# Two key tiles to a step: regrouped attention and turned mean squares in the first layer of a three-part kernel

## The chip, the cores and the metric

The kernel runs on one core of a Trainium2 chip. A core has a matrix engine (TensorE, PE in the profile, with its weight loads listed apart as PEld), three engines for element-wise work (VectorE or DVE, ScalarE or ACT, GpSimd or POOL) and a queue engine (SyncE, SP) that issues the transfers here. Each engine takes its instructions in order. Operands lie in the on-chip memory SBUF, matrix products in the small memory PSUM, of eight banks.

The metric is the device time of one execution in microseconds (us); several executions are summed up by their median. A profile is one further execution with every instruction recorded; its own time is given beside it.

## The reference, cut to what matters

The input is x, 8 batches of 256 channels on a 32 x 32 grid (1024 positions). Three parts follow: layer 0 (attention over the grid plus a gated convolution network with an 8 x 8 FFT filter), layer 1's causal attention, and layer 1's eight experts. Only layer 0 is touched, and the place where it hands over to layer 1:

```python
def _ln(x, w, b):
    r = lax.rsqrt(jnp.mean(x * x, axis=1, keepdims=True) + LN_EPS)
    return x * r * w[:, None, None] + b[:, None, None]

# attention: 4 heads, keys of 32, values of 64 channels
qkv = _bn(_conv1x1(x, qkv_w), ...)
attn = softmax(einsum('bhkn,bhkm->bhnm', q, k) * SCALE)
out = einsum('bhdm,bhnm->bhdn', v, attn) + _bn(_dwconv3(v_img, pe_w), ...)
return _bn(_conv1x1(out, proj_w), ...)

# EDFFN
x = _dwconv3(_conv1x1(x, pi_w), dw_w)        # 1024 channels
x = gelu(x1) * x2                            # 512 channels
x = _conv1x1(x, po_w)
x = irfft2(rfft2(8x8 patches of x) * fft_p)

# layer 0
x = x + gamma1 * attention(_ln(x, norm1))
x = x + gamma2 * edffn(_ln(x, norm2))
```

All is in float32.

## The kernel before, in words

**Engines and order.** All of layer 0's compute goes through the wrapper `InOrder` (line 59; the recorded call is line 69, which is why every row of the profile says L69). Each engine runs in the order in which the program text issues its instructions, so the weaving described below decides what stands behind what. Rows are told apart by their tiles.

**Tiles.** PSUM is divided into `ps_s` (two tiles of two banks, tag s: the scores `s`, the products `pz`, and some of `pq` and `pp`), `ps_o` (the attention's `po` and `sums`) and `ps_m` (two banks in turn, tag mm, for all the rest).

**The pieces of one batch's work.** The names are those of the profile's tiles.

- `rms_norm` (line 571) makes the normed input `xn`, in two halves of 512 positions. ACT squares (`sq`). PE multiplies each 128 positions of the squares, as the stationary operand, with a column `mean_1` (`ms`, 16 instructions a half). ACT copies to `y`, POOL makes the power -0.5, one Newton step and a split into two parts (`a`, `y`, `r`, a chain on 128x4). PE transposes (`tr`), ACT copies (`rT`), PE spreads the row over all partitions (`rbn`), and DVE multiplies (`xn`).
- `queries_keys` (line 649): norm1, then the products `pq` for queries and keys, split by ACT into a high part `hi` and by DVE into a rest `lo`. `stack` (line 671) copies these parts, one transfer of 128 KB for each head and part, into `qst` and `kst`, in which the high and low parts of a head's 32 channels lie on 128 partitions; one matmul then gives the score to full precision.
- `values` (line 684): `pq` again, `vfull`, transposes `tpv` into `vT`, and the padded picture `vpad`.
- `v_conv` (line 714): the 3 x 3 convolution of the values on DVE, 16 "taps" of 128x1024 into `o`.
- `attend` (line 723): four chunks of 256 queries times eight key tiles of 128 keys. Each step makes one key tile's `s` (4 matmuls, one per head) and its exp `pT` (ACT), then the products `po` and `sums` of the key tile before it. po and sums write 32 columns each, four instructions beside one another on column tiles of the array. When a chunk is complete, `close` copies its results and returns a list of later steps, taken one to a key tile: `invert` (DVE reciprocal `sr`), `split` (ACT `rh`, POOL `rl`), `spread` (PE `rb`; DVE two operations, pu and o).
- `finish` (the last chunk's steps) and `project` (line 813): products `pp`, added to the residual `t` by DVE.
- `hidden` (line 884): the EDFFN's first part for the batch before: `ph` on PE, the padded `hpad` on ACT, eight taps of 128x1024 on DVE for each of eight groups (tiles `x` and `conv`), gelu on ACT, and the product `hid` on DVE (two rows to a group).
- `spectrum` (line 975), for the batch two before: `pz` from `hid`, `zf`, `pf` (the DFT), `gf` (DVE filter), `py` (inverse) and the DVE addition to `t`.

**The order.** `main_of(i)` weaves generators: the head is norm2(i-1) alternating with spectrum(i-2), and one step of the head's weave in every three is followed by a step of attend(i); the rest of attend(i) is woven with queries_keys(i+1), one step of it to every two of attention; then finish, gelu, stack, values(i+1) and project(i). `together` runs this main chain beside a side chain, v_conv(i) followed by hidden(i-1), choosing between them by the sums of the numbers that each generator yields: a yield is an estimate of the us of the work since the last, and the chain that is behind goes next. For i = 1 and 7 the side's numbers are scaled by 0.75.

Two places in a steady batch are used as marks. One is the point at which `pz` starts again for spectrum(i-2) after its wait for the last `hid`; the other is the `rb` of chunk 2, behind which DVE has the o update, a run of taps, the reciprocal of chunk 3 and the last `hid` products.

Of the kernel before, what the change touches and what calls it, by code (L numbers as in the profile page):

```python
# [18 lines left out]
P = 128  # L19
B, C, H, W = 8, 256, 32, 32  # L20
N = H * W
# [34 lines left out]
NVEC = _n  # L56

# [17 lines left out]
def conv_attn_hybrid_kernel(  # L75
# [29 lines left out]

    vec = const.tile([P, NVEC], F32, name="vec")
    nc.sync.dma_start(vec, vecs)

    def col(name, i=0, n=1):
        o, w = _VOFF[name]  # L110
        assert i + n <= w
        return vec[:, o + i : o + i + n]
# [6 lines left out]
    mean_1 = const.tile([P, 1], F32, name="mean_1")  # L119
    nc.gpsimd.memset(mean_1, 1.0 / C)  # L120

# [310 lines left out]
    with ExitStack() as l0:  # L432
# [97 lines left out]
        pick_n = wpool.tile([2 * nq, nq, P], F32R, name="pick_n")  # L530
        pickn = one.tile([2 * nq, nq, P], F32, tag="full", name="pickn", bufs=2)
        nc.gpsimd.memset(pickn, 0.0)
        for half in range(2):
            nc.gpsimd.affine_select(
                out=pickn, in_=pickn, compare_op=ALU.not_equal, fill=1.0, base=-nq * half,
                pattern=[[-1, nq], [0, P]], channel_multiplier=1,
            )
        nc.gpsimd.tensor_copy(pick_n, pickn)
        mhalf = const.tile([P, nq], F32, name="mhalf")
# [6 lines left out]
        def padded(name):  # L546
            p = one.tile([P, H + 2, W + 2], F32, tag=name, name=name)
            nc.gpsimd.memset(p, 0.0)
            return p

# [3 lines left out]
        def interior(p, h):  # L554
            r = H // 2
            return p[:, 1 + h * r : 1 + (h + 1) * r, 1 : 1 + W]
# [4 lines left out]
        def tap(dst, p, w, k):  # L561
            src = p[:, k // 3 : k // 3 + H, k % 3 : k % 3 + W]
# [6 lines left out]
        def rms_norm(b, wname, xn):  # L569


            sq_of, r_of, rT_of = {}, {}, {}

            def squares(h):
                sq_of[h] = []
                for k in range(KC):
                    sq = one.tile([P, HALF], F32, tag="full", name="sq", bufs=2)
                    act.activation(sq, t[b][:, k, h * HALF : (h + 1) * HALF], AF.Square)
                    sq_of[h].append(sq)

            def factors(h):
                ms = ps_m.tile([P, nq], F32, tag="mm", name="ms")
                for k, sq in enumerate(sq_of.pop(h)):
                    for i in range(nq):
                        pe.matmul(
                            ms[:, i : i + 1], sq[:, i * P : (i + 1) * P], mean_1,
                            start=(k == 0 and i == 0), stop=(k == KC - 1 and i == nq - 1),
                        )
                y = small.tile([P, nq], F32, tag="y", name="y")
                act.activation(y, ms, AF.Identity, bias=eps_rms)  # L590

                r = r_of[h] = small.tile([P, 2, nq], F32, tag="r", name="r")
                a = small.tile([P, nq], F32, tag="a", name="a")
                pool.tensor_tensor(a, y, mhalf, ALU.pow)
# [4 lines left out]
                pool.tensor_copy(r[:, 0, :].bitcast(F32R), a)  # L599
                pool.tensor_sub(r[:, 1, :].bitcast(F32R), a, r[:, 0, :])  # L600

            def turned(h):
                tr = ps_m.tile([2 * nq, P], F32, tag="mm", name="tr")
                pe.transpose(tr, r_of.pop(h).rearrange("p a b -> p (a b)"), ident)
                rT_of[h] = small.tile([2 * nq, P], F32R, tag="rT", name="rT", bufs=2)
                act.copy(rT_of[h], tr)

            def apply(h):
                rT = rT_of.pop(h)
                rb = ps_m.tile([P, HALF], F32, tag="mm", name="rbn")  # L610
                for i in range(nq):
                    pe.matmul(rb[:, i * P : (i + 1) * P], pick_n[:, i, :], rT, start=True, stop=True)
# [6 lines left out]
            factors(0)  # L619
            squares(1)  # L620
            yield 2.0
            factors(1)
            yield 2.0
            turned(0)
            yield 0.2
            apply(0)
            turned(1)
            yield 1.0
            apply(1)
            yield 1.0  # L630
# [21 lines left out]
        def queries_keys(b):  # L652
# [7 lines left out]
            for g in range(2):  # L660
                hi = one.tile([P, N], F32R, tag=f"hi{g}", name="hi")
                lo = one.tile([P, N], F32, tag=f"lo{g}", name="lo")
# [7 lines left out]
                att[b][g] = (hi, lo)  # L670
# [1119 lines left out]
```

## Time and profile before

| what | value |
|---|---|
| median of 3 runs | 3320.35 us (3318.31 to 3326.01) |
| the profiled execution's own time | 3326.09 us |
| its span in the profile | 3324.3 us |
| mean granted TensorE clock | 0.969 |
| layer 0 | 0 to about 1444 us |
| layer 1's attention, then the experts | to about 2080 us, then to the end |
| PE, DVE, ACT, POOL busy | 94%, 72%, 43%, 10% |
| transfers | 113.85 MB, mean 34 GB/s |

The span runs from the first instruction to the last; 1.8 us of the profiled execution lie around it. A row of the timeline is a run of equal instructions: start, duration, engine, line, operation, output<-inputs, shapes, count, and in brackets how long the engine had been idle just before and what it waited for. Since matmuls overlap, the starts of successive PE rows say more than their durations. A row of windows gives, for a stretch of time, each engine's busy time with its number of instructions, then the granted TensorE clock as a share of full speed, the share of the transfer engines and GB/s.

### The profile page before, as it was taken

To read this page: it belongs to the slowest core of one execution; us is meant where nothing else is said; L and a number is where in the kernel's file an instruction comes from. 1 tells how busy PE (TensorE), PEld (TensorE's weight loads), DVE (VectorE), ACT (ScalarE), POOL (GpSimd) and SP (SyncE) were. 2 spreads that over 40 slices of the span, in tenths; PEclk is the share of its full clock that TensorE was granted. 3 is DMA by queue.
4 is the path that set the end of the run, shared out by engine and by line. 5 is a ranking of instruction groups with operands and counts; after the bars stand their busy time and mean duration, and the time that the engine had idled before them with its cause. 6 is when DMAs were issued, how large, how long until landed. Compare 5 with 4: busy or idle time off the path is not lost.

```text
span 3324.3 us, 43278 instructions
## 1 busy us (share of the span) xinstructions
PE 3108.8 (94%) x17366; PEld 2108.0 (63%) x17366; DVE 2395.9 (72%) x3710; ACT 1417.6 (43%) x2185; POOL 328.9 (10%) x530
## 2 busy tenths in 40 slices
PE   6998999999999998769999998999999999999999
PEld 4554646464656555345556666687878777878787
DVE  2369788878787887744554444688888877888887
ACT  2545454555454544313333332344444444444443
POOL 1120101020202010001222222400000000000000
PEclk9989999999999999879999999899999999999999
DMA  4112020202020200030111101100000000000000
GB/s 121 29 24 51 26 52 26 51 27 51 27 51 26 52 14 7 16 134 13 51 47 43 39 26 45 45 25 21 20 20 20 24 18 26 23 20 26 13 7 13
DMA packets 42918, 113.85 MB, mean 34 GB/s; under 512 B 6406, under 2 KB 14550, under 8 KB 38870
## 3 DMA queue, kind: packets, MB, share of 16 engines
q1 hardware_dynamic: 42710, 111.01, 11.0%
q8 instruction: 139, 2.28, 0.3%
q14 instruction: 69, 0.57, 0.1%
HBM read 43.61 MB, written 33.82 MB: 23 GB/s over the span
## 4 chain that ended last, share of the span: by engine, by line
PE 50%; DVE 4%; ACT 1%; POOL 1%; issue 0%; DMA 0%; POOLq 0%; ACTq 0%; SPq 0%; DVEq 0%
PE pm L69 12%; PE pa L69 12%; PE q L69 11%; PE s L69 5%; PE po L69 3%; PE pv L69 2%; PE pk L69 2%; DVE zt L69 1%; DVE nm L69 1%; PE tpt L69 1%; DVE pr L69 1%; PE tp L69 1%; ACT pr L69 1%; PE tpz L69 1%; PE pw L69 1%
## 5 line engine op out<-in xcount | busy, mean ns | idle before, releaser
L69 ACT ACTIVATE h<-h,bn_o,bn_s 128x512 f32<-128x512 f32 x384 | 308.7, 813 | 632.5 <-DVE h L69 632.4
L69 DVE SCALAR_TENSOR_TENSOR conv<-hpad,vec,conv 128x1024 f32<-128x1024 f32 x256 | 331.4, 1300 | 14.7 <-ACT conv L69 8.9
L69 DVE SCALAR_TENSOR_TENSOR x<-hpad,vec,x 128x1024 f32<-128x1024 f32 x248 | 321.6, 1300 | 23.5 <-ACT x L69 17.4
L69 ACT ACTIVATE pT<-s 128x1024 f32<-128x1024 f32 x256 | 261.6, 1024 | 150.3 <-PE s L69 150.1
L69 PE MATMUL pm<-h,w 128*128 128x512 f32 (+1 forms) x768 | 318.1, 523 | 0.0
L69 PE MATMUL po<-pT,vT 128*32 128x256 f32 x4096 | 276.5, 388 | 6.5 <-ACT pT L69 4.8
L69 PE MATMUL ph<-xn,piw 128*128 128x512 f32 x512 | 246.1, 608 | 3.1 <-DVE gf L69 1.1
L69 PE MATMUL s<-kk,z 128*128 128x512 f32 x512 | 242.4, 601 | 0.6 <-DVE pr L69 0.6
L69 PE MATMUL s<-qst,kst 128*128 128x256 f32 x1024 | 217.9, 335 | 6.1 <-DMA kst<-lo 5.9
L69 PEld LDWEIGHTS s<-qst,kst 128*128 128x128 f32 x1024 | 147.8, 192 | 88.8 <-issue 72.2
L69 PEld LDWEIGHTS pm<-h,w 128*128 128x128 f32 x768 | 146.7, 191 | 75.6 <-issue 62.1
L69 DVE TENSOR_TENSOR h<-h,wb 128x1024 f32<-128x1024 f32 x128 | 156.8, 1225 | 43.2 <-ACT h L69 43.2
L69 DVE TENSOR_TENSOR h<-pa,first 128x512 f32<-128x512 f32 x128 | 88.3, 690 | 134.9 <-PE pa L69 131.4
L69 DVE SCALAR_TENSOR_TENSOR o<-vpad,pe_w,o 128x1024 f32<-128x1024 f32 x128 | 163.3, 1281 | 24.1 <-ACT o L69 21.2
L69 ACT ACTIVATE hpad<-ph,pi_o 128x512 f32<-128x512 f32 x126 | 87.0, 691 | 211.7 <-PE ph L69 207.2
L69 DVE TENSOR_TENSOR h<-h,first 128x256 f32<-128x256 f32 x384 | 164.3, 428 | 13.2
L69 PEld LDWEIGHTS po<-pT,vT 128*32 128x32 f32 x4096 | 107.7, 109 | 88.7 <-ACT pT L69 8.3
L69 PEld LDWEIGHTS ph<-xn,piw 128*128 128x128 f32 x512 | 90.8, 190 | 108.9 <-issue 92.1
L69 PE MATMUL sums<-pT,ones 128*32 128x256 f32 x2048 | 158.8, 382 | 0.0
L69 PE MATMUL pz<-pow__118,hid 128*128 128x256 f32 x512 | 129.8, 408 | 29.1 <-DVE hid L69 29.1
L69 PE MATMUL pa<-tz,ws 128*128 128x256 f32 x512 | 156.0, 387 | 0.0
L69 PE MATMUL pa<-ze,w 128*128 128x256 f32 x512 | 153.8, 383 | 0.0
(258 smaller groups left out, 5940.3 us busy)
## 6 DMA issues: line engine op xcount, KB each, us to landing
t<-in_x_dram SPq DMA_DIRECT2D x8, 1024.0 KB, 7.5
qst<-hi SPq DMA_DIRECT2D x64, 128.0 KB, 2.3
qst<-lo SPq DMA_DIRECT2D x64, 128.0 KB, 2.3
kst<-hi SPq DMA_DIRECT2D x64, 128.0 KB, 2.3
kst<-lo SPq DMA_DIRECT2D x64, 128.0 KB, 2.3
td<-t SPq DMA_DIRECT2D x8, 1024.0 KB, 3.8
t<-td SPq DMA_DIRECT2D x8, 1024.0 KB, 4.9
ze<-zd SPq DMA_DIRECT2D x16, 512.0 KB, 4.1
```

The costliest lines, as they stand in the source:

```text
L69: return self._tc.keep_in_program_order(method(*args, **kwargs))
```

## The change

1. `attend` takes two key tiles to a step: both `s` tiles and both exps are issued, then the products of the two key tiles before them. `pT` gets four buffers instead of two. A chunk's later steps come one to a step of two tiles, so the list loses its empty places. The yields become 3.5 and 2.6.
2. `rms_norm`: the squares are now the moving operand and 32 columns of ones the stationary one, in four column tiles for the four 128-position parts, so that mean squares of both halves stand in one bank as rows, each repeated over 32 partitions. ACT scales and copies this block (`yr`, 128x256, in `level`), PE transposes its halves (`tpy`), one ACT copy takes one column per part (`y`), and one POOL chain on 128x8 serves both halves. One pair of `tr`, one `rT`, then both `rbn` and the four DVE products follow together. norm2 has one more empty step ahead of `tr`.
3. `hi` and `lo` have one buffer each for both groups; their parts go to DRAM (four writes of 512 KB a batch) and `stack` reads them back in eight transfers of 512 KB.
4. The padded pictures have rows of 33 instead of 34 columns, one column of zeros serving as the right border of a row and the left one of the next.
5. `vec`, the table of small parameters, is loaded in two parts. The second, with the parameters of the experts, is loaded behind layer 0, and its batch-norm factors are computed there too, instead of at the start.
6. The weave constants: the head gives attention a step every 6 instead of every 3, queries_keys a step to each step of attention (of two tiles now) with one instead of two empty steps ahead; v_conv's yield in `hidden` is 1.7 instead of 1.5.

The steps a steady batch issues on DVE keep their number, but not their places. Behind the o update of chunk 2, DVE's order held, before, 16 taps, the reciprocal, the o update of chunk 3, three pairs of hid products and one pair of additions of pp ahead of the last pair of hid; after, 20 taps and two pairs of additions.

The diff, cut to its core:

```diff
-    vec = const.tile([P, NVEC], F32, name="vec")
-    nc.sync.dma_start(vec, vecs)
+    vec = const.tile([P, NVEC0], F32, name="vec")
+    nc.sync.dma_start(vec, vecs[:, :NVEC0])
...
-            p = one.tile([P, H + 2, W + 2], F32, tag=name, name=name)
+            p = one.tile([P, (H + 2) * (W + 1) + 2], F32, tag=name, name=name)
...
-            src = p[:, k // 3 : k // 3 + H, k % 3 : k % 3 + W]
+            src = inside(p, k // 3, k % 3, H)
...
+            def means(h):
+                if h == 0:
+                    of["ms"] = ps_m.tile([P, 2, P], F32, tag="mm", name="ms")
+                for k, sq in enumerate(of.pop(h)):
                     for i in range(nq):
                         pe.matmul(
-                            ms[:, i : i + 1], sq[:, i * P : (i + 1) * P], mean_1,
-                            start=(k == 0 and i == 0), stop=(k == KC - 1 and i == nq - 1),
+                            of["ms"][i * KD : (i + 1) * KD, h, :], ones[:, :KD], sq[:, i * P : (i + 1) * P],
+                            start=(k == 0), stop=(k == KC - 1),
                         )
+            def level():
+                of["yr"] = one.tile([P, 2, P], F32, tag="yr", name="yr")
+                act.activation(of["yr"], of.pop("ms"), AF.Identity, bias=eps_rms, scale=1.0 / C)
+
+            def factors():
+                yr = of.pop("yr")
+                tp = ps_m.tile([P, 2, P], F32, tag="mm", name="tpy")
+                for h in range(2):
+                    pe.transpose(tp[:, h, :], yr[:, h, :], ident)
+                y = small.tile([P, 2, nq], F32, tag="y", name="y")
+                act.copy(y, tp[:, :, ::KD])
...
             squares(0)
             yield 0.2
-            factors(0)
+            means(0)
             squares(1)
-            yield 2.0
-            factors(1)
-            yield 2.0
-            turned(0)
+            yield 1.0
+            means(1)
+            level()
+            yield 1.0
+            factors()
+            yield 1.0
+            for _ in range(gaps):
+                yield 1.0
+            turned()
             yield 0.2
             apply(0)
-            turned(1)
-            yield 1.0
             apply(1)
-            yield 1.0
+            yield 2.0
...
-                att[b][g] = (hi, lo)
+                parts = att[b][g] = [dram.tile([P, N], F32, tag=f"part{g}{r}", name="part", bufs=2) for r in range(2)]
+                for part, src in zip(parts, (hi, lo)):
+                    nc.sync.dma_start(part, src.bitcast(F32))
...
-                    for hd in range(NH):
-                        nc.sync.dma_start(
-                            st[r * KD : (r + 1) * KD, hd, :].bitcast(F32), src[hd * KD : (hd + 1) * KD, :].bitcast(F32)
-                        )
+                    nc.sync.dma_start(
+                        st[r * KD : (r + 1) * KD].bitcast(F32), src.rearrange("(h k) n -> k h n", k=KD)
+                    )
...
-                return [None, invert, None, split, None, None, spread]
+                return [invert, split, None, spread]
...
+                for j0 in range(0, nj, 2):
+                    new = []
+                    for j in (j0, j0 + 1):
+                        ks = slice(j * P, (j + 1) * P)
+                        s = ps_s.tile([P, NH, QC], F32, tag="s", name="s")
+                        for hd in range(NH):
+                            pe.matmul(s[:, hd, :], kst[:, hd, ks], qst[:, hd, qs], start=True, stop=True)
+                        pT = two.tile([P, NH, QC], F32, tag="pT", name="pT", bufs=4)
+                        act.activation(pT, s, AF.Exp)
+                        new.append((po, sm, j, pT, c))
+                    products()
+                    late.extend(new)
                     later()
-                    yield 1.75
+                    yield 3.5
...
-            yield from rms_norm(b, "n2w", xn2[b])
+            yield from rms_norm(b, "n2w", xn2[b], 1)
...
-                yield 1.5 * us
+                yield 1.7 * us
...
-                yield from weave(head, steps, 3, rest=False)
-            yield from weave(steps, later_on(2, queries_keys(i + 1)) if i + 1 < B else none(), 2)
+                yield from weave(head, steps, 6, rest=False)
+            yield from weave(steps, later_on(1, queries_keys(i + 1)) if i + 1 < B else none(), 1)
```

## The prediction

> **What bounds the kernel now.** I read the page first, then windows by stage, then PE and DVE row by row inside one batch, then the ends of waits. The page gives TensorE most of the span and VectorE three quarters:
>
> ```profile
> span 3324.3 us, 43278 instructions
> ...
> PE 3108.8 (94%) x17366; PEld 2108.0 (63%) x17366; DVE 2395.9 (72%) x3710; ACT 1417.6 (43%) x2185; POOL 328.9 (10%) x530
> ```
>
> That mean hides two kinds of stretch. Layer 0 ends near 1444 us and repeats every 163.65 us (the same DVE row at 475.14 and 638.78). The windows (start:end, length, busy time of PE, PEld, DVE, ACT, POOL, then clock, DMA share, GB/s) cut one batch, i=3, at two marks: pz restarting after its wait for hid, and the rb of chunk 2.
>
> ```profile
> 501.96:631.86 129.90, 126.08 (x1107) 76.44 (x1107) 104.42 (x98) 66.84 (x100) 20.08 (x31) 1.00 0.05 17
> 631.86:665.61 33.75, 28.69 (x127) 14.56 (x123) 31.27 (x32) 18.24 (x30) 0.84 (x1) 0.90 0.55 125
> ```
>
> For 129.90 us PE is the bound (it waits 3.8 us, DVE 25). In the next 33.75 us, the transition, DVE is the bound (idle 2.5): it finishes the side work on which the next pz depends. So time saved on PE counts in the first, and VectorE work pushed past the mark counts in full in the second. Batch 1 (DVE 58.64 of 60.00 us from 240 on) is DVE's; i=0 (PE 80.49 of 81.00 from 72 on) is PE's.
>
> PE's rows show a key tile (start, duration):
>
> ```profile
> 586.59 0.74 PE L69 MATMUL s<-qst,kst 128*128 128x256 f32 x4
> 587.26 1.07 PE L69 MATMUL po<-pT,vT 128*32 128x256 f32 x16
> 588.15 0.61 PE L69 MATMUL sums<-pT,ones 128*32 128x256 f32 x8
> 588.70 1.99 PE L69 MATMUL ph<-xn,piw 128*128 128x512 f32 x4
> ...
> 633.00 1.07 PE L69 MATMUL po<-pT,vT 128*32 128x256 f32 x16
> 633.89 0.61 PE L69 MATMUL sums<-pT,ones 128*32 128x256 f32 x8
> 634.32 1.05 PE L69 MATMUL po<-pT,vT 128*32 128x256 f32 x16
> 635.18 0.61 PE L69 MATMUL sums<-pT,ones 128*32 128x256 f32 x8
> 635.73 1.98 PE L69 MATMUL ph<-xn,piw 128*128 128x512 f32 x4
> ```
>
> Starts matter: s to po 0.67, po to sums 0.89, sums to the next kind 0.55, together 2.11 us; at 633 two products stand together, and there sums to po takes 0.43.
>
> Last, what a wait at pz does. Batch 2 restarts at 332.04 after 3.41 us; batch 7 after 0.69:
>
> ```profile
> 332.04 4.63 PE L69 MATMUL pz<-pow__118,hid 128*128 128x256 f32 x10 [3.41 <-DVE hid L69]
> 336.46 3.41 PE L69 MATMUL ms<-mean,sq 128*128 128x1 f32 x16
> ```
> ```profile
> 1158.11 2.42 PE L69 MATMUL pz<-pow__118,hid 128*128 128x256 f32 x10 [0.69 <-DVE hid L69]
> 1160.37 1.84 PE L69 MATMUL ms<-mean,sq 128*128 128x1 f32 x16
> ```
> ```profile
> 332.10:345.10 13.00, 13.00 (x41) 0.50 0.00 0
> 332.04:346.30 14.26, 14.26 (x46) 0.55 0.00 0
> 1158.11:1166.08 7.97, 7.97 (x46) 1.00 0.01 2
> ```
>
> The same 46 matmuls take 14.26 us in place of 7.97: after the wait the granted clock (third figure from the right) is 0.50 for 13 us. That is 6.3 us lost in a PE-bound stretch, and batch 2 (332.04 to 501.96) is 169.92 long, 6.27 over the period.
>
> **The change part by part, per steady batch.**
>
> *Steps of two tiles.* A pair costs 2 x 2.11 = 4.22 us. Afterwards: s to s 0.46 (estimate: 4 instructions at the 0.115 us between the starts of the three rb at 632.08, 632.19 and 632.31, of the same shape), s to po 0.67, then 0.89 + 0.43 + 0.86 + 0.55 as at 633; 3.86, so 0.36 saved; bounds 0.15 (only the 633 rows) and 0.42. The exps (1.02 us each) get two more pT buffers, so products wait less for ACT. 14 of a batch's 16 pairs lie before the mark: -5.0 (-2.1 to -5.9). One more s stands ahead of the mark: +0.45.
>
> *Mean squares.* A half is 16 instructions in 1.84 us (1160.37). Now 32 ones are loaded instead of 128 squares, and 16 instructions run in four column tiles of 128 columns; nearest is sums, 8 instructions with 256 columns in 0.43 to 0.55. I take 0.85 (0.6 to 1.2): four halves a batch (norm2, and norm1 of the next), -4.0 (-2.6 to -5.0). Two added transposes per norm at 0.14 us (tpv's 273 ns rows overlap, four in 0.44-0.6): +0.55. mean_1's memset goes, once.
>
> *The norm's chain.* ms goes through level (128x256 on ACT, some 0.4 us, ss's row), tpy, the copy y, and one POOL chain of 128x8 for both halves; tr waits for POOL on PE, with s, products, rbn and pz queued behind it. Rows of the old chains:
>
> ```profile
> 506.45 2.08 POOL L69 TENSOR_TENSOR a<-y,mhalf 128x4 f32<-128x4 f32 x1 [16.66 <-ACT y L69]
> ...
> 513.49 1.01 POOL L69 TENSOR_TENSOR a<-y,mhalf 128x4 f32<-128x4 f32 x1
> ...
> 517.94 0.20 POOL L69 TENSOR_TENSOR r<-a,r 128x4 fp32r<-128x4 f32 x1
> ```
>
> 7.0 and 4.65 us beside DVE's taps; without them 2.66 (570.58 to 573.24). The 128x8 pow is 1.67 us (layer 1, 1464.01) against 1.01, so 3.3 quiet, 5.3 to 7.8 beside taps; I take 6.4. Behind y, PE has pz(2) (3.5) but only once the first exp frees an s tile, then pf: some 3.1 us of cover. tr waits 3.3 (2 to 4.7). The third pf waits about 1.0, others 1.0; the stretch's waits go from 3.8 to 5.3: +1.5.
>
> So the PE-bound stretch changes by -5.0 + 0.45 - 4.0 + 0.55 + 1.5 = -6.5, to 123.4.
>
> *DVE behind the mark.* The weaves' constants and v_conv's 1.5 to 1.7 reorder DVE's program order. Before, 16 taps follow chunk 2's o update; after, 20, and one more pair of t<-pp stands ahead of the last hid: 4 x 1.28 + 1.4 - 1.2 (fewer waits inside) = +5.3 (4 to 6.5), transition 39.1. DVE loses that work in a stretch where it has 25 us to spare, so nothing comes back. PE's pp ends near 32, six pz follow, and pz then waits for hid about 5.4 us instead of 0.7.
>
> *The clock.* 5.4 us is longer than the 3.41 that halved the clock at 332, so I expect it at every restart. Lost: pz's ten 4.63 - 2.42 = 2.2, then, with the slow ms gone, part of the next sixteen pz (5.6 against 3.6) before the clock returns: I take 3.4 (0 if no drop; 6.3 as at 332).
>
> The Trainium skill, TensorE: Matmul & The Clock Gate, section "What's actually happening", lets the full clock return after one busy window of some 3.4 us. By it a restart would lose about 1.7 us (an estimate from that page) and the sum below would be 9 us lower; the 13 us at 332 contradict it, and I go by the trace.
>
> *Stacking.* 4 writes of 512 KB and 8 reads instead of 32 copies of 128 KB, all on SP's queue. In the loop s(i+1) starts 48 us after them: hidden; without that cover some 10 us. hi and lo have one buffer, so group 1 waits for group 0's writes (2.8 us for 512 KB). At the start it is open:
>
> ```profile
> 71.12 3.36 PE L69 MATMUL s<-qst,kst 128*128 128x256 f32 x8 [5.91 <-DMA kst<-lo]
> ```
>
> 2 MB at the 208 GB/s of that copy against writes landing and 2 MB at the 400 to 420 of a DRAM read, one landing more, the buffer's wait, and -1.8 for the norm: 0 (-5 to +5).
>
> *Little or nothing:* 33-column pads (every tap is 1.28 us, at each of the three column offsets); level's larger ACT row (ACT is busy 51% of that stretch); vec's second part as one more DMA on SP's queue behind layer 0 (8 KB of wrs beside it land in 2.5 us) and the moved bn fold, one ACT table load of 1.28 us and ten small rows: +0.5 at layer 1's start, up to 4 if PE finds nothing else there.
>
> **Sum.** Start 0; i=0: 15 pairs x 0.36 and 2 halves x 1.0, -7.5; i=1, DVE-bound, -1; i=2: -6.5 + 5.3 + 3.4 - 6.3 (its halved clock is there already) = -4.1; i=3 to 6: 4 x (-6.5 + 5.3 + 3.4 = +2.2) = +8.8; i=7, DVE-bound from 1192 on, part of its slow restart: +2; norm2 at the end -2; layer 1 +0.5. Total -3.3. The profiled execution took 3326.1 (span 3324.3 and 1.8 around it), so 3322.8; it lies 5.7 above the median of the runs, 3320.35, from which the forecast is 3317: gain and loss cancel.
>
> **Rivals.**
> *A, slower: the halved clock stays.* Place: pz's restart in i=3 to 7. If it holds for 13 us as at 332, a restart loses 6.3, not 3.4: 5.5 x 2.9 = +16, 3333. Beyond 5.2 us per restart it passes the measurement's bound. For it: row 332.04. Against: in the transition at 652.2 half clock ended after 6.8 us, and ms, at half clock 3.41 of those 13 us, shrinks.
> *B, faster: no drop.* If pz's wait stays short enough for full clock (pp ending later than 32 on a half clock of its own): -3.4 x 5.5 = -19, 3298. For it: 0.7 us now leaves the clock full; against: 3.41 did not.
> *C, faster: the transition does not lengthen,* because DVE runs those taps in waits I have not seen: -5.3 x 5 and with it B, about 3272. Against: DVE idles 2.5 us there.
>
> **How the numbers follow.** Forecast 0.40, A 0.27, B 0.23, C 0.10. The median of three runs spans 0.2%, 6.6 us, about what a measurement can tell from no change. Within the forecast's case the pair saving alone moves the sum by 0.2 x 88 pairs = 18 us one way, 5 the other, and tr's wait by 8 either way, so it spreads 0.12 faster, 0.17 same, 0.11 slower (own range 3300 to 3335). A is slower; B nearly all and C faster, a few hundredths of B same: faster 0.42, same 0.20, slower 0.38. The low end takes in B and half of C, 3279; the high end A with a chain at 7.8, 3341.
>
> **What would show it.** s, s, po, sums, po, sums in 3.86 us; ms halves of 0.85; PE's wait of tr on POOL near 3.3 (at 0 the stretch is shorter still, at 6 A's side wins); pz's wait on hid near 5.4 and clock 0.50 behind it; the two windows 123.4 (126.8 with the slow restart) and 39.1; a period near 166. It is wrong if pz restarts at full clock, if s after s does not come at 0.46, or if DVE idles behind the mark.

## The result and the profile after

The changed kernel takes 3329.52 us (median of 16 runs, 3323.6 to 3333.57) against 3320.53 us before (median of 16 runs, 3317.87 to 3326.79): a ratio of 1.0023, 95% interval 1.0015 to 1.0030. It is slower by 9 us; forecast was 3 us less, 3317, in a range from 3279 to 3341. The profiled execution took 3330.36 us, with a span of 3328.6.

The page of the changed kernel, its span and engines:

```profile
span 3328.6 us, 43001 instructions
...
PE 3044.8 (91%) x17398; PEld 2072.1 (62%) x17398; DVE 2396.7 (72%) x3710; ACT 1407.1 (42%) x2168; POOL 276.1 (8%) x417
```

PE is busy 64 us less than before, VectorE (DVE) as long as before, and the span is longer. So the time went into waiting or a slower clock, or it moved to where nothing was changed. The same two stretches of batch 3, in windows (start:end, length, busy time of PE, PEld, DVE, ACT, POOL, granted clock, DMA share, GB/s):

```profile
500.15:623.24 123.09, 118.39 (x1111) 73.13 (x1111) 98.86 (x92) 63.02 (x94) 12.76 (x17) 0.98 0.11 39
623.24:663.11 39.87, 29.36 (x127) 14.55 (x123) 36.87 (x37) 20.91 (x32) 0.95 (x1) 0.90 0.48 95
```

The PE-bound stretch fell from 129.90 to 123.09 us, the transition rose from 33.75 to 39.87. This batch is 162.96 us against 163.65: nearly nothing gained, as forecast, though not with the forecast's sizes.

PE's timeline from that restart on (start, duration, operation, in brackets the idle time before it and its releaser):

```profile
500.15 4.64 PE L70 MATMUL pz<-pow__116,hid 128*128 128x256 f32 x10 [5.07 <-DVE hid L70]
504.72 0.76 PE L70 MATMUL ms<-sq,ones 128*32 128x128 f32 x16
505.41 3.72 PE L70 MATMUL pz<-pow__116,hid 128*128 128x256 f32 x16
509.06 0.64 PE L70 MATMUL ms<-sq,ones 128*32 128x128 f32 x16
509.63 1.12 PE L70 MATMUL pf<-zf,dft 128*128 128x512 f32 x2
...
518.01 0.38 PE L70 MATMUL tr<-ident,r 128*8 128x128 f32 x2 [0.80 <-POOL r L70]
...
540.80 1.19 PE L70 MATMUL s<-qst,kst 128*128 128x256 f32 x8
541.93 1.07 PE L70 MATMUL po<-pT,vT 128*32 128x256 f32 x16
542.82 0.61 PE L70 MATMUL sums<-pT,ones 128*32 128x256 f32 x8
543.25 1.05 PE L70 MATMUL po<-pT,vT 128*32 128x256 f32 x16
544.11 0.61 PE L70 MATMUL sums<-pT,ones 128*32 128x256 f32 x8
544.65 0.70 PE L70 MATMUL ph<-xn,piw 128*128 128x512 f32 x1
```

Four things are to be seen. A pair of key tiles now takes 544.65 - 540.80 = 3.85 us (3.86 forecast, 4.22 before). A half of ms takes 0.57 us from its start to the next row's (0.85 forecast, 1.84 before). pz waits 5.07 us for hid (5.4 forecast), and its ten matmuls then take 4.64 us, the 4.63 of a halved clock. tr waits 0.80 us for POOL, not 3.3. Windows of the same stretch show how long the clock stays halved (third figure from the right): to about 505, and no further.

```profile
500.15:505.00 4.85, 4.85 (x18) 3.47 (x22) 4.74 (x5) 0.18 (x1) 0.00 (x0) 0.50 0.00 0
505.10:512.00 6.90, 6.83 (x60) 5.03 (x48) 3.25 (x4) 4.22 (x7) 0.00 (x0) 1.00 0.00 0
```

POOL's timeline says for the most part why tr waits so little: its chain is 517.96 - 513.63 = 4.33 us long here, where 6.4 was taken.

```profile
513.63 1.87 POOL L70 TENSOR_TENSOR a<-y,mhalf 128x8 f32<-128x8 f32 x1 [34.73 <-ACT y L70]
...
517.76 0.20 POOL L70 TENSOR_TENSOR r<-a,r 128x8 fp32r<-128x8 f32 x1
```

In these two profiles the first layer got shorter. Layer 1's first transpose starts at 1448.72 us, before at 1457.37. (How far the two are typical is taken up below: in a second profile of the kernel before that row starts at 1450.15.) From there on both kernels issue the same matmuls, and yet the changed one ends 4.3 us later: 13 us were lost in code that the change leaves alone, 7.5 of them in the experts. A half batch of them, from one row te<-te,qs on VectorE to the next, takes 74.19 us before and 74.54 after. VectorE's timeline shows where, before first, then after:

```profile
2356.84 2.61 DVE L69 TENSOR_TENSOR qs<-qs 128x512 f32<-128x512 f32 x5
```
```profile
2355.31 0.69 DVE L70 TENSOR_TENSOR qs<-qs 128x512 f32<-128x512 f32 x1
2356.45 1.82 DVE L70 TENSOR_TENSOR qs<-qs 128x512 f32<-128x512 f32 x4 [0.46 <-DVE qs L70]
```

Of five dependent rows, the second starts 0.46 us after the first has ended, where in the kernel before it starts 0.10 us after it. This recurs in each of the 12 regular half batches. The row waits for nothing that the profile shows: the first row, whose result it needs, ended at 2356.00, and ScalarE's copy that it reads ended at 2355.13.

### The profile page after: what moved, and what is told of

It reads as the page before. It is cut to its first block, busy times and chain, and to the rows that moved or that the text cites. A ratio compares the mean times of both kernels' runs of the same rounds, so it can differ in the third digit from the quotient of the medians.

```text
span 3328.6 us, 43001 instructions
## 1 busy us (share of the span) xinstructions
PE 3044.8 (91%) x17398; PEld 2072.1 (62%) x17398; DVE 2396.7 (72%) x3710; ACT 1407.1 (42%) x2168; POOL 276.1 (8%) x417
## 4 chain that ended last, share of the span: by engine, by line
PE 50%; DVE 4%; ACT 1%; POOL 1%; issue 0%; DMA 0%; SPq 0%; ACTq 0%; POOLq 0%; DVEq 0%
PE pm L70 12%; PE pa L70 12%; PE q L70 11%; PE s L70 5%; PE po L70 3%; PE pk L70 2%; PE pv L70 2%; DVE zt L70 1%; DVE nm L70 1%; PE tpt L70 1%; DVE pr L70 1%; PE tp L70 1%; ACT pr L70 1%; PE tpz L70 1%; PE pw L70 1%
## 5 line engine op out<-in xcount | busy, mean ns | idle before, releaser
L70 ACT ACTIVATE pT<-s 128x1024 f32<-128x1024 f32 x256 | 248.1, 1025 | 67.6 <-PE s L70 67.6
L70 PE MATMUL pz<-pow__116,hid 128*128 128x256 f32 x512 | 140.5, 432 | 65.0 <-DVE hid L70 60.7
L70 PE MATMUL s<-qst,kst 128*128 128x256 f32 x1024 | 181.4, 321 | 13.5 <-DMA kst<-part 13.3
L70 PEld LDWEIGHTS po<-pT,vT 128*32 128x32 f32 x4096 | 120.4, 110 | 88.6 <-issue 7.2
L70 PEld LDWEIGHTS s<-qst,kst 128*128 128x128 f32 x1024 | 139.8, 195 | 55.9 <-issue 52.4
L70 PEld LDWEIGHTS pz<-pow__116,hid 128*128 128x128 f32 x512 | 108.0, 217 | 94.5 <-DVE hid L70 66.7
```

What stands on the lines that cost most here:

```text
L70: return self._tc.keep_in_program_order(method(*args, **kwargs))
```

## The experiments

Twelve kernels ran, each beside runs of the kernel before on the same chip. "After" is the changed kernel.

### Fewer taps behind the mark, all groups alike

```diff
-together(main_of(i), hidden(i - 1, v_conv(i), pace=PACE if i in (1, B - 1) else 1.0), SIDE)
+together(main_of(i), hidden(i - 1, v_conv(i), pace=PACE if i in (1, B - 1) else 0.92), SIDE)
```

> Edit: in the steady batches (i = 2 to 6) the hidden taps count 0.92 of their time in the weave, so 16 taps instead of 20 stand behind chunk 2's o update, as in the kernel before. Theory A (the longer DVE run behind the mark and the halved clock at pz's restart eat the gain of the PE-bound stretch): the transition falls from 39.9 to about 34 us, pz's wait from 4.4-5.2 to under 1.5, no half clock behind it, the PE-bound stretch from 123 to about 120; 8 to 9 us a batch, five batches, 3330 to about 3288. Theory B (DVE is the bound of the whole batch once PE is quicker, the taps only move): under 15 us in all, with new DVE waits named by PE inside the stretch.

Measured: 3319.20 us, ratio to before 0.9995 (0.9985 to 1.0004). In the first layer the edit won nothing: layer 1 starts at 1449.75 (after: 1448.72), though the transition fell to 31.2 us and pz's wait vanished. The stretch grew to 131 to 132 us. PE's timeline names the new wait:

```profile
747.50 3.75 PE L70 MATMUL ph<-xn,piw 128*128 128x512 f32 x4 [4.99 <-DVE xn L70]
```

The taps went ahead of norm1's four xn, whose rbn hold both banks that ph needs. Neither theory fits whole: the run behind the mark went as A said, and the new wait of 5 us is the one by which B is known. The 10 us that this kernel is faster than after lie behind the first layer: in the profiles 3.3 us in layer 1's attention and 11.2 in the experts, where its half batches take 74.19 us. Of the 11.2, 4.9 stand ahead of the first te row, a part that varies between executions (see the account at the end).

### Is it VectorE's place in its stream of instructions?

```diff
         s2, o2 = bn_fold("g2", "be2", "m2", "v2", eps_moe, "bn2", extra="b2")
+        spare = hp.tile([P, 1], F32, name="spare", bufs=1)
+        dve.memset(spare, 0.0)
```

In the changed kernel:

> Edit: the changed kernel with one VectorE instruction more (a memset of one column) ahead of the experts. Theory A (each half batch of the experts takes 74.54 instead of 74.19 us because VectorE's instruction stream, exactly 128 instructions to a half batch, is shifted by one place and a stall in the supply of instructions meets two dependent qs rows): the period goes back to 74.19 in all or nearly all half batches, -4.6 us, 3325. Theory B (the 0.35 us come from where buffers lie, or from the relative phase of the engines): 74.54 stays, 3329 to 3330.

Measured: 3325.84 us, 1.0018 (1.0009 to 1.0028), half batches 74.54. In the kernel before:

> Edit: the kernel before with the same one instruction more ahead of the experts. Theory A: the period of a half batch changes from 74.19 to 74.54 if the stall comes at every second place, or stays at 74.19 if it comes at few places; the first layer is as before. Theory B: 74.19 stays. Besides, a second profile of this first layer and of layer 1: if the windows of halved clock in layer 1 depend on the execution and not on the kernel, their lengths and the time from layer 1's first transpose to the experts (615 us before, 621 after) differ from the first profile's by some us.

Measured: 3320.20 us, 1.0006 (0.9997 to 1.0016), half batches 74.19. By itself this spoke for theory B. But a memset that takes over another instruction's wait makes the separate wait instruction superfluous: counted with those, neither stream had become longer. So neither edit tested the theory, and two memsets were needed, which move everything behind them by exactly one:

```diff
+        spare0 = hp.tile([P, 1], F32, name="spare0", bufs=1)
+        dve.memset(spare0, 0.0)
+        spare1 = hp.tile([P, 1], F32, name="spare1", bufs=1)
+        dve.memset(spare1, 0.0)
```

> Edit: the changed kernel with two one-column memsets ahead of the experts. In the first try the one memset took the place of a separate wait instruction, so that VectorE's stream had as many instructions as without it; counted with those waits, this edit moves the experts' part by exactly one. Over six kernels the 74.54 us half batches are those in which the second qs row stands at a place that leaves 1 when divided by 4 (3977 and so on in the changed kernel), the 74.19 us ones at 0, 2 and 3. Theory A (place in the stream): now at 3978, so 74.19 throughout, the experts 1236.8 to some 1226 to 1231, the whole 3329.5 to 3322. Theory B (anything else): 74.54, no gain.

Measured: 3323.62 us, 1.0008 (0.9999 to 1.0017); half batches 74.18. And in the kernel before:

> Edit: the kernel before with the same two memsets, which move the second qs row from 4012 to 4013 (remainder 1). Theory A: the half batches of the experts become 74.54, 13 of them and +4.6 us, with the longer step between the halves as in the changed kernel up to +6.5: 3325 to 3327, though nothing of the first layer is touched. Theory B: 74.19, 3320.

Measured: 3327.64 us, 1.0021 (1.0010 to 1.0031); half batches 74.53. One instruction more cures the changed kernel and makes the old one as slow as the changed one. VectorE's timelines, the changed kernel with two memsets, then the kernel before with them:

```profile
2352.81 2.61 DVE L70 TENSOR_TENSOR qs<-qs 128x512 f32<-128x512 f32 x5
```
```profile
2351.90 1.82 DVE L69 TENSOR_TENSOR qs<-qs 128x512 f32<-128x512 f32 x4 [0.46 <-DVE qs L69]
```

The two memsets also write eight bytes of SBUF, which might shift other buffers. So the eight bytes alone, in one memset:

```diff
+        spare = hp.tile([P, 2], F32, name="spare", bufs=1)
+        dve.memset(spare, 0.0)
```

> Edit: the changed kernel with one memset of two columns, that is with the eight bytes of the two memsets' tiles in SBUF, but with VectorE's stream no longer than in the changed kernel. It tells the two readings of the shift by two memsets apart. Theory A (place in the stream of instructions): half batches of 74.54 us. Rival (where the experts' buffers lie): 74.18.

Measured: 3327.44 us in one run; half batches 74.54, and the row waits again:

```profile
2353.59 1.82 DVE L70 TENSOR_TENSOR qs<-qs 128x512 f32<-128x512 f32 x4 [0.45 <-DVE qs L70]
```

So it goes with the stream and not with these eight bytes. The kernel before shows the same without any edit. Its first te step stands 127 instructions ahead of the second, not 128, so its qs rows stand one place further on in a block of 128, the place to which the two memsets moved all the others. In VectorE's timeline of that kernel it waits, while the steps behind it do not:

```profile
2208.11 0.69 DVE L69 TENSOR_TENSOR qs<-qs 128x512 f32<-128x512 f32 x1
2209.25 1.82 DVE L69 TENSOR_TENSOR qs<-qs 128x512 f32<-128x512 f32 x4 [0.46 <-DVE qs L69]
```

Which places stall was tried with five memsets in place of two:

> Edit: the changed kernel with five memsets ahead of the experts, VectorE's stream four places on (the second qs row at 3981, remainder 1 of 4). Theory A1 (the stall comes at every fourth place): half batches of 74.54 us, as at 3977. Theory A2 (only at some places of a longer block, which would also explain that the single-tile kernel at 3969 had none): 74.18. In both the first layer is as in the changed kernel.

Measured: 3322.20 us in one run; 74.19. Remainder 1 does not decide; A1 is out. The kernel with the pair steps undone, below, was expected at 74.54 by the same rule and also took 74.19.

The kernel before with one memset gave something else: a second profile of its first layer, which the memset leaves alone. The windows of batch 2, from pz's restart to rb of chunk 2, in the first profile and in this one:

```profile
332.04:468.21 136.17, 132.36 (x1106) 81.44 (x1106) 104.49 (x98) 65.44 (x98) 17.92 (x31) 0.95 0.04 17
```
```profile
332.27:463.85 131.58, 127.77 (x1106) 77.62 (x1107) 104.49 (x98) 65.37 (x98) 19.67 (x31) 0.99 0.05 17
```

The same matmuls, 4.6 us apart, by the granted clock. pz had waited 3.41 us in both, but the clock stayed halved for 13.7 us in the first and for 3.4 in the second, where the ten matmuls took 4.11 us and the ms behind them ran at full clock again:

```profile
332.27 4.11 PE L69 MATMUL pz<-pow__118,hid 128*128 128x256 f32 x10 [3.41 <-DVE hid L69]
336.22 1.84 PE L69 MATMUL ms<-mean,sq 128*128 128x1 f32 x16
```

The two memsets in the kernel before gave a third profile, 131.56 us. So the 13 us at half clock, from which the prediction took 6.3 us, were no part of every execution: in the second profile batch 2 takes 165.33 us, 1.7 more than the 163.64 of the batches behind it, and not 6.3. The first profile was of a run of 3326.09 us, and four of before's 16 runs lie at 3325.5 to 3326.8, the others under 3322.7.

### The start: two queues

```diff
-                    nc.sync.dma_start(
+                    queue = nc.scalar if b == 0 and r % 2 else nc.sync
+                    queue.dma_start(
```

> Edit: the changed kernel, where batch 0's eight reads of the parts are issued from two queues (every second from ScalarE's), so that two groups of 32 partitions are written at a time. Theory A (the start is later because a read into 32 partitions moves 205 GB/s): first s at 70 to 72 us instead of 77.4, 3324. Theory B (the rate is that of the transfer engines as such): first s stays at 76 to 78, 3330.

Measured: 3323.60 us, 1.0007 (0.9997 to 1.0017). PE's timeline has the first s at 76.83, after at 77.44:

```profile
76.83 2.05 PE L70 MATMUL s<-qst,kst 128*128 128x256 f32 x8 [2.53 <-DMA kst<-part]
```

Windows of this kernel show 324 GB/s from 58 to 64 us and 207 GB/s from 66 to 74, with both queues at work in both stretches; so a second queue does not by itself bring the higher rate, and what made the difference is open. The end of the reads hardly moved; those of the keys were issued at 60.75 us instead of 58.23. So theory A's remedy brings the first s no nearer. The whole came out at A's 3324 all the same, which the first s doesn't give: in the profile batch 2 takes 162.23 us instead of 165.07, behind a wait at pz of 7.3 us instead of 10.1, and the rest is open. Half batches are 74.54, as in the changed kernel.

### Taps early, where VectorE idles

```diff
-                    yield 1.3 * pace
+                    yield 1.3 * pace * (0.5 if m < 2 and pace == 1.0 else 1.0)
```

> Edit: the changed kernel, where in batches 2 to 6 the taps of the first two hidden groups count half in the weave; four more taps stand ahead of chunk 0's reciprocal, where VectorE idles 5.2 us, three more ahead of its o update, 10 instead of 20 behind chunk 2's, and ahead of norm1's xn none more than four. Theory A (the loss is the run of taps behind the mark and the slow restart it brings, and the first try at it failed because its taps went ahead of norm1's xn, for which ph waited 5.0 us): transition 30 to 32 us, no wait at pz, no half clock behind it, the stretch 121 to 125; a period of 152 to 157 instead of 163, 3280 to 3300. Theory B (VectorE's taps cost the same wherever they stand): ph's wait for xn is again 4 us or more, the stretch 130 or longer, the period 162 to 164. By its place in the stream (3971, remainder 3) the experts should take 74.19.

Measured: 3295.17 us, 0.9918 (0.9902 to 0.9934). The period is 157 us. Windows and PE's timeline of this kernel at a restart (there is no gap any more: sixteen pz follow pp directly, and the mark at 650.78 is the seventh of them):

```profile
650.78:776.57 125.79, 121.08 (x1120) 73.70 (x1118) 109.70 (x101) 68.84 (x102) 12.50 (x17) 0.99 0.10 38
776.57:807.64 31.07, 26.07 (x118) 13.29 (x115) 26.21 (x27) 17.88 (x28) 1.16 (x1) 0.89 0.61 121
```
```profile
640.48 9.17 PE L70 MATMUL pp<-o,projw 128*128 128x512 f32 x16
649.48 3.62 PE L70 MATMUL pz<-pow__116,hid 128*128 128x256 f32 x16
653.03 0.64 PE L70 MATMUL ms<-sq,ones 128*32 128x128 f32 x16
653.60 3.72 PE L70 MATMUL pz<-pow__116,hid 128*128 128x256 f32 x16
657.25 0.64 PE L70 MATMUL ms<-sq,ones 128*32 128x128 f32 x16
```

The second ms starts 6.47 us behind the mark; in the changed kernel it was 509.06 - 500.15 = 8.91, and 9.3 a batch later. That is the price of the halved clock by itself: 2.3 to 2.8 us in four of the changed kernel's restarts from batch 3 on, and 1.5 in the fifth (826.45), where the clock was back 2.8 us after the restart. VectorE's work moved into the stretch (109.70 us busy there instead of 98.86) and did not delay it by as much. The stretch is 2 to 3 us longer all the same: eight ph instructions, some 4 us of PE, moved along with the taps (60 in the stretch instead of 52). ph's wait for xn did not come, and the trace has 12 taps behind chunk 2's o update, ahead of the last hid, not 10. Theory A holds, but for the stretch, which is a little over its 125.

### The pair steps undone

```diff
-                for j0 in range(0, nj, 2):
-                    new = []
-                    for j in (j0, j0 + 1):
+                for j in range(nj):
...
-                    products()
-                    late.extend(new)
+                    if late:
+                        product(*late[:4])
...
-                return [invert, split, None, spread]
+                return [None, invert, None, split, None, None, spread]
...
-                yield from weave(head, steps, 6, rest=False)
+                yield from weave(head, steps, 3, rest=False)
```

> Edit: the changed kernel with the attention of the kernel before (one key tile to a step, two pT buffers, the old list of later steps, the weave's 3, 2 and 2), all the rest as changed: norm, stacking, pads. It takes the pair steps away alone. The prediction's terms: the PE-bound stretch longer by 14 x 0.36 = 5.0 less the one s that goes behind the mark (0.45), so 123 to 127.5; the transition with 19 taps behind the mark 38 to 39, the drop at pz's restart stays; a period of 166, the whole some 30 us above the changed kernel if nothing else gives way, 3355. Rival (pairs save nothing, the norm does it all): period 163, 3330. The half batches of the experts 74.54 (3969, remainder 1) by the theory of the place.

Measured: 3378.68 us, 1.0171 (1.0153 to 1.0189): 49 us above the changed kernel, not 25, and half batches of 74.19. The period is 172 to 175 us. The stretch is 7 to 11 us longer, of which the prediction's figure for the pairs makes 4.6; norm1's tr waits longer for POOL, and s and the products after it run on a halved clock (PE's timeline in batch 4):

```profile
773.25 0.59 PE L70 MATMUL tr<-ident,r 128*8 128x128 f32 x2 [5.41 <-POOL r L70]
773.49 1.20 PE L70 MATMUL s<-qst,kst 128*128 128x256 f32 x4
774.62 1.94 PE L70 MATMUL po<-pT,vT 128*32 128x256 f32 x16
```

In the changed kernel that tr waits 1.33 us. The transition is 41.9: VectorE's timeline has 20 taps in it, not the 19 expected, and a wait of 3.62 us for ScalarE. pz waits 6.1 to 6.7 us.

```profile
831.68 1.29 DVE L70 TENSOR_TENSOR hid<-x,conv 128x512 f32<-128x512 f32 x2 [3.62 <-ACT x L70]
```

The period rules out the rival's 163, but the test is not clean, since tr's wait and the halved clock behind it came along. That the pairs save 0.36 us each is read from the rows of the two kernels (4.22 and 3.85); this run doesn't measure it apart.

### The norm undone

```diff
-        def rms_norm(b, wname, xn, gaps=0):
-            ... # means, level, factors for both halves
+        def rms_norm(b, wname, xn):
+            ... # factors(0), factors(1) with mean_1, two chains of 128x4
-            yield from rms_norm(b, "n2w", xn2[b], 1)
+            yield from rms_norm(b, "n2w", xn2[b])
```

> Edit: the changed kernel with the old norm (mean squares by 16 loads of squares a half, two chains of 128x4), all the rest as changed. By the profile a half of ms takes 1.84 us in place of 0.6, four to a batch, 5.0 us; the added transposes (2 x 0.4) and the wait of tr for POOL (2.1) go: stretch 123 to about 126. The order then puts 17 taps instead of 20 behind the mark, so the transition falls to about 36. Theory A (both terms as such): period 162 to 163, about the changed kernel's time, 3325 to 3333. Rival (the norm is worth nothing, tr's wait on POOL takes what ms gives): stretch 123 or less, period 159, 3305 to 3312.

Measured: 3353.46 us, 1.0103 (1.0086 to 1.0120). The stretch is 127.3 to 127.8 us in batches 2 to 4 and 131.2 in 5 and 6; the transition did not fall to 36 but stayed at 39.3, and the period is 167 to 170.6. So the new norm is worth 4.3 to 4.6 us in batches 3 and 4 (2.1 in batch 2), where 3 were expected (126). The total missed its bracket above all because the transition kept its taps: VectorE's timeline has 19 of them, not 17, and a longer wait for ScalarE.

```profile
640.11 1.30 DVE L70 TENSOR_TENSOR hid<-x,conv 128x512 f32<-128x512 f32 x2 [2.14 <-ACT x L70]
```

With that the transition follows the prediction's sum in both kernels that undo a part. The changed kernel's 39.87 us hold 20 taps and 1.6 us of idle time. One tap of 1.28 us less and 0.5 us more idle give 39.1 here (39.3 measured); as many taps and 2.0 us more idle give 41.9 in the kernel with single steps (41.9 measured). PE's timeline behind a restart of this kernel:

```profile
665.77 4.63 PE L70 MATMUL pz<-pow__118,hid 128*128 128x256 f32 x10 [4.70 <-DVE hid L70]
670.20 2.29 PE L70 MATMUL ms<-mean,sq 128*128 128x1 f32 x16
672.35 3.70 PE L70 MATMUL pz<-pow__118,hid 128*128 128x256 f32 x16
```

In batches 5 and 6 the half clock held longer (13.7 us instead of 6.8, behind waits of 4.6 us), which makes the other 3.4 us.

### The start: old stacking for batch 0

On top of the early taps:

```diff
+                if b == 0 and g == 1:
+                    hi = two.tile([P, N], F32R, tag="hid", name="hi", bufs=ng + 1)
+                    lo = two.tile([P, N], F32, tag="hid", name="lo", bufs=ng + 1)
...
+                if b == 0:
+                    att[b][g] = (hi, lo)
+                    continue
...
+                    if b == 0:
+                        for hd in range(NH):
+                            nc.sync.dma_start(
+                                st[r * KD : (r + 1) * KD, hd, :].bitcast(F32), src[hd * KD : (hd + 1) * KD, :].bitcast(F32)
+                            )
+                        continue
```

> Edit: the kernel with the early taps, and in batch 0 alone the old stacking, straight from SBUF with 32 copies, the keys' parts in buffers that hid uses later. Theory A (the start is late by the 2 MB of writes, since the reads run at the 205 to 220 GB/s of the copies): first s back at 71 to 73 instead of 77.8, 5 us less, 3290; VectorE's place in the experts (3982) is one not yet seen, and could cost up to 6.5. Theory B (the start is late for another reason, such as keys waiting for the shared buffers): first s at 76 to 78, 3295.

Measured: 3289.80 us, 0.9909 (0.9892 to 0.9925), the lowest here, though its interval overlaps that of the early taps alone; in the profiles layer 1 begins 4.7 us sooner than with those. Half batches are 74.19. PE's timelines, this kernel and the changed one:

```profile
71.01 2.51 PE L70 MATMUL s<-qst,kst 128*128 128x256 f32 x4 [5.88 <-DMA kst<-lo]
```
```profile
77.44 2.04 PE L70 MATMUL s<-qst,kst 128*128 128x256 f32 x8 [13.26 <-DMA kst<-part]
```

The edit also gives the keys' parts buffers of their own, so by itself it doesn't part the two theories. VectorE's timelines do. The keys' last lo is made at 55.42 us in the changed kernel, in spite of a wait, and at 55.21 in the kernel before:

```profile
54.01 1.41 DVE L70 SCALAR_TENSOR_TENSOR lo<-pq,qkv_o,hi 128x512 f32<-128x512 f32 x2 [3.32 <-ACT hi L70]
```
```profile
54.46 0.75 DVE L69 SCALAR_TENSOR_TENSOR lo<-pq,qkv_o,hi 128x512 f32<-128x512 f32 x1 [0.97 <-ACT hi L69]
```

So the keys were not late (theory B), and the transfers were: the reads from DRAM into 32 partitions run, from 60 us on, at about the rate of the copies they replace, and the writes come on top. Theory A holds for the cause, if not for the remedy tried first.

## Why the prediction was right and wrong

The table takes the kernel before from its second profile (one run of 3320.14 us, near the median), cut at the same events: the first s, the last rb of batch 0, the seventh pz of the restarts, layer 1's first transpose, the experts' first pw, the end. The last column is the changed kernel with one memset of one column, whose first layer is the same and whose half batches also take 74.54 us: the changed kernel seen a second time.

| part | forecast | measured | seen again |
|---|---|---|---|
| start, to the first s | 0 | +5.7 | +5.7 |
| batch 0 | -7.5 | -8.8 | -8.8 |
| batch 1 | -1 | +6.0 | +6.0 |
| batch 2 | +2.2, and -6.3 credited | -0.3 | -0.3 |
| batches 3 to 6 | +8.8 | -3.4 | -0.1 |
| batch 7 and the end of layer 0 | 0 | -0.6 | -0.6 |
| layer 1 | +0.5 | +1.1 | -0.1 |
| experts | 0 | +10.6 | +5.6 |
| sum | -3.3 (without the credit +3.0) | +10.2 | +7.4 |

**Right.** The mechanism of layer 0: a PE-bound stretch that shrinks, a VectorE-bound transition that grows, a longer wait at pz and a halved clock behind it. The pair (3.85 against 3.86), the transition (39.87 against 39.1) and pz's wait (4.4 to 5.2 against 5.4) came as worked out, and so did batch 0; the restart's price was below its term (1.5 to 2.8 against 3.4).

**Wrong in size.** ms costs 0.57 a half, not 0.85, and tr's wait in norm2 0.8, not 3.3: the stretch without its slow restart is some 120.7 us, not 123.4, and batch 3 comes out at -0.7, not +2.2. Batch 1, put down as "DVE-bound, -1", has the same reordering: 27 taps instead of 22 behind its mark, 5 x 1.28 = 6.4 us, and no PE-bound stretch to pay for them. At the start the reads were costed at the 400 to 420 GB/s of another transfer; from 60 us on they run at some 210. These errors nearly cancel, and that is luck: without the credit layer 0 was forecast at +2.5 and measured at -1.4 and +1.9.

**Wrong in kind, twice: the steps that failed.** First, "i=2: ... - 6.3 (its halved clock is there already)". That loss was in the profiled execution; in the second profile batch 2 loses 1.7 us, so 4.6 of the credit were subtracted from a median that never had them. The two profiles of the kernel before differ by 5.9 us, and these 4.6 are the largest single part of it (the rest of the first layer makes 2.6, layer 1 -4.4, the experts +3.1). They were counted once in the profile's distance from the median and once as a gain.

Secondly, the sum stopped at "layer 1 +0.5" and put the experts at nothing, as code that the change doesn't touch. Moving VectorE's instructions by one place costs the experts 12 x 0.35 = 4.2 us (the expectations counted 13). The step between the two halves of the batches took 85.6 us instead of 83.6, 2.0 more, and goes with the place as well: the two memsets bring it to 83.6 in the changed kernel and to 85.4 in the kernel before. Together that is 6.2 us; by the ratios of the runs the two memsets take 5 us off the changed kernel and put 7 on the kernel before. What sets the step is not settled: it was 81.9 and 85.1 in other kernels with half batches of 74.19.

The rest of the experts' 10.6 in the third column, 4.4 us, lies ahead of the first te row: that part was 112.4 or 117.4 us in profiles of the changed kernel's code and 112.7 to 116.1 in those of the kernel before, the longer ones with a further 3 to 7 us of halved clock. It varies on both sides, as batches 3 to 6 do, where one restart's half clock held for 3.4 us in some profiles and for 6.8 in others. Both are left out of the account: -3.3 + 4.6 + 6.2 = +7.5, against +9.0 measured, whose interval is 5 to 10.

Of the rivals, A (half clock for 13 us at each restart) gives nearly the measured time, but by a mechanism that did not come: the clock was back before the second row of pz, which took 3.72 us. That A was near in value is chance. B and C needed a pz that waits little; only the kernels with fewer taps behind the mark showed that.

## What to carry to other kernels

When work of a second engine must be moved off a stretch where it holds up the first, look for the place where that second engine idles (here 5.2 us ahead of the first reciprocal) and put the work there, not merely elsewhere. Before a loss in a profile is entered as a gain, see it in a second profile, above all where the granted clock is behind it. And when code ahead of an unchanged, fully unrolled part changes, compare that part's period too: here one instruction more or less decided 5 to 7 us, most of the 9 by which the change lost.

## What the runs showed of the hardware

- VectorE's second qs row starts 0.46 us behind the first or 0.10, depending on how many VectorE instructions, waits included, stand ahead of it; each half batch has exactly 128, so it recurs in every one. Counted in the traces, the late row of the changed kernel is VectorE's instruction 2303 and every 128th from there, and one kernel more, with the old stacking for batch 0, stalls at 2303 - 128 = 2175, in its first step. Kernels built on the changed one that have the row at 2293, 2295 to 2297, 2302, 2304 or 2307 don't stall. In the kernel before the late row is 2305 with two memsets and 2177 = 2305 - 128 without an edit, and 2304 is not late. So every stall seen stands at one place in a block of 128, another one in each family of kernels; why there is open. A stall in the supply of instructions would do this, but the profile shows no such event.
- The granted clock halves after a wait of 3.41 us at pz in all three profiles of the kernel before, but for how long differs from one execution to the next at the same instruction: 13.7, 3.4 and 3.4 us; ten pz took 4.63, 4.11 and 4.11 us, and the stretch was 136.17, 131.58 and 131.56. After waits of 4.4 to 5.2 us it cost the changed kernel 1.5 to 2.8 us.
- DRAM reads that fill 32 partitions each moved 207 to 214 GB/s from one queue, as SBUF copies did (208); with two queues at work it was 324 for 6 us and 207 for the 8 us from 66 on.

The Trainium skill's rule from TensorE: Matmul & The Clock Gate, section "What's actually happening" (full clock after one busy window of some 3.4 us), would have made a restart cost about 1.7 us, an estimate. Batch 2 of the second profile lost that much (165.33 against 163.64 us). The changed kernel's restarts cost 1.5 to 2.8, which lies between the rule's 1.7 and the 3.4 that the prediction took; the 13.7 us of halved clock in the first profile, and in batches 5 and 6 of the kernel with the old norm, are longer than the rule gives.
